# A graph-network kernel's first block held in program order, with fixed steps for projecting, rooting and turning each group of rows

## The chip, the core and the metric

The kernel runs on one core of one Trainium2 chip. The metric is the device time of one execution in microseconds (us), as a median of several. Inside the core five engines work side by side, each through its own queue: TensorE (PE) multiplies matrices, VectorE (DVE) and ScalarE (ACT) work on elements, GpSimd (POOL) does next to nothing here, and SyncE (SP) issues the transfers between main memory and the core's own memory. Results of TensorE land in PSUM[...] from where DVE or ACT take them.

## What is computed

Four layers of graph attention over 3327 nodes with 256 features and one adjacency matrix; each layer is added to its input and normalised. The last layer has three attention stages inside. The change touches only the first layer:

```python
def _L0_gnn_ref(features, adj, Wq, Wk):
    Qn = _cos_normalize(features @ Wq.T)     # rows of 128, divided by their length
    Kn = _cos_normalize(features @ Wk.T)
    raw_att = Kn @ Qn.T
    att = jnp.where(adj > 0, raw_att, NEG) * TEMP
    att = jax.nn.softmax(att, axis=1)
    prop_fea = att @ features
    adj_mask = (jnp.sum(adj, axis=1) > 0).astype(features.dtype)[:, None]
    prop_fea = adj_mask * prop_fea + (1.0 - adj_mask) * features
    return (1.0 - KEEP_RATIO) * prop_fea + KEEP_RATIO * features
...
x = _layernorm(x + _L0_gnn_ref(x, adj, L0_gnn_Wq, L0_gnn_Wk), axis=-1)
```

## The kernel before

**Tiling.** The nodes are padded to 3328 and cut into 26 tiles of 128 (NT) and 7 blocks of 512 (NB; the last has 256). Six layers in the kernel's count (the last layer's three stages apart) each run over blocks b, and inside a block over tiles j (the loop at L908; one turn of it is called a step). Step j of a block multiplies the weights e of tile j (128 rows by the block's 512 columns) with the values V of tile j, in eight matmuls that add up over j in four PSUM tiles `po` (L946). A softmax's denominator comes from a column of ones in V.

**Weights.** They are made two steps ahead (LA = 2) by `make`. For layer 0, `weights0(b, j)` (L429) does, for even j, `take_adj`, which turns two tiles of the adjacency matrix from int32 into a mask of bytes (L386) and adds them to a running sum (L392, L396), and `load_adj`, which loads the next pair into one of three slots called `stage`. Then one product `ps` (L435), its exp on ACT (`ex`, L444), and on DVE exp times mask (`e`, L424). Rows of 128 of the normalised keys and queries, transposed, lie in `FT[g]`: ps for tile j needs half 0 of group g = j // 4 and half 1 of group b.

**Preparing FT.** `prep0(g)` (L280) is a generator that prepares a group of four tiles, and its `yield`s cut it into parts that the loop places:
- projecting: four products `pqk` on PE (16 matmuls, L305), copied to `qk` by DVE or, for groups 1 and 2, ACT (L315, L317);
- squares and their sums (L296 on DVE, L300 on ACT);
- rooting: the inverse square root of eight sums a row by a guess and three Newton steps, twelve short DVE instructions (L328 and `rsqrt`, L130 to L139, result `rn`);
- scaling: half 0 on ACT (L338), half 1 on DVE (L340);
- turning: eight transposes `pqkT` on PE (L346), half 1 before half 0, each half copied into FT on ACT (L350; for group 0 half 1 on DVE, L348).

During block 0 of layer 0 all of this happens between the steps; later blocks find FT complete. `sum_adj` (L400) closes a block's adjacency sum at step 23.

**Order.** A scheduler decides the order of instructions on each engine. Inside a region opened at L68, the instructions of PE, ACT, DVE and POOL stay in the order in which the program states them; SP isn't in the list:

```python
start = tc.manual_schedule(
    engines={engines.PE, engines.Activation, engines.DVE, engines.Pool}
)
```

The region ends after the fourth step (L954). From there on the scheduler may move instructions, such as masks of later tiles, ahead of others, as far as data and slots allow. PSUM has three banks for everything but `po` (tag `pb`), stage has three slots, `e` five and `ex` three, `xT` two.

The parts of a group are placed by the lines L915 to L944: in the third step of four, group g + 1's x is loaded and the group after it projected and squared; in the first two of the next four steps it is rooted with scaling, and turned. The tile that needs a newly turned group first is made one step later.

Of the kernel before, what the change touches and what calls it, by code (L numbers as in the profile page):

```python
# [8 lines left out]
F32 = mybir.dt.float32  # L9
# [8 lines left out]
P = 128  # L18
D = 256
H = 128  # L20
# [11 lines left out]
def gnn_stack(ctx: ExitStack, tc: tile.TileContext, a: dict, N: int, out: bass.AP):  # L32
# [14 lines left out]
    def bw(b):  # L47
        return min(CH, NP - b * CH)
# [227 lines left out]
    def load_x(g):  # L276
        for t in tiles_of(g):
            nc.sync.dma_start(V[0][t][:, :D], a["x"][t * P : (t + 1) * P, :])

    def prep0(g):  # L280

        wd = bw(g)
        xT = xTs[g]
        ts_ = tiles_of(g)
        ss = cols.tile([P, 2, 4], F32, tag="ss", name="ss")
        if len(ts_) < 4:
            nc.vector.memset(ss, 1.0)
        qks = []

        def squares(k):  # L290
            for i in range(2):
                s = qks[k][:, i * H : (i + 1) * H]
                c = ss[:, i, k : k + 1]
                jk = work.tile([P, H], F32, tag=f"sq{i}", name=f"sq{i}", bufs=1)
                if g < 2 and i == 1:
                    nc.vector.tensor_tensor_reduce(  # L296
                        jk, s, s, 1.0, 0.0, ALU.mult, ALU.add, c
                    )
                else:
                    nc.scalar.activation(jk, s, AF.Square, accum_out=c)  # L300

        for k, t in enumerate(ts_):
            pm = bank("pqk")
            for h in range(2):
                nc.tensor.matmul(  # L305
                    pm[:, : 2 * H],
                    xT[:, h, k * P : (k + 1) * P],
                    w["qk"][:, h, :],
                    start=(h == 0),
                    stop=(h == 1),  # L310
                )
            tag, bufs = ("y", 6) if g % 2 else ("qk", 4)
            qk = work.tile([P, 2 * H], F32, tag=tag, name="qk", bufs=bufs)
            if g in (1, 2):
                nc.scalar.copy(qk, pm[:, : 2 * H])  # L315
            else:
                nc.vector.tensor_copy(qk, pm[:, : 2 * H])  # L317
            qks.append(qk)
            if g == 0:
                squares(k)  # L320
        yield
        if g > 0:
            for k in range(len(ts_)):
                squares(k)
            yield

        sf = ss.rearrange("p i k -> p (i k)")
        nc.vector.tensor_scalar(sf, sf, COS_EPS * COS_EPS, None, ALU.max)  # L328
        rn = cols.tile([P, 8], F32, tag="rn", name="rn")
        rsqrt(rn, sf, 8)  # L330
        if g == 1:
            yield
        for k in range(len(ts_)):
            for i in (1, 0):
                s = qks[k][:, i * H : (i + 1) * H]
                c = rn[:, 4 * i + k : 4 * i + k + 1]
                if i == 0:
                    nc.scalar.mul(s, s, c)  # L338
                else:
                    nc.vector.tensor_scalar(s, s, c, None, ALU.mult)  # L340
        yield
        for i in (1, 0):
            pt = bank("pqkT")
            for k, t in enumerate(ts_):
                s = qks[k][:, i * H : (i + 1) * H]
                nc.tensor.transpose(pt[:, k * P : (k + 1) * P], s, ident)  # L346
            if i == 1 and g == 0:
                nc.vector.tensor_copy(FT[g][:, i, :wd], pt[:, :wd])  # L348
            else:
                nc.scalar.copy(FT[g][:, i, :wd], pt[:, :wd])  # L350


    masks = {}
# [4 lines left out]
    def mask(b, j, n=1):  # L358
        wd = bw(b)
        return masks[b][:, j * wd : (j + n) * wd]  # L360
# [21 lines left out]
    def take_adj(b, j):  # L382

        wd = bw(b)
        st = stages.pop((b, j))[:, : 2 * wd]
        nc.vector.tensor_scalar(mask(b, j, 2), st, 0, None, ALU.is_gt)  # L386
        if j == 0:
            adj_sum[b] = st
        elif j == 2:
            acc = work.tile([P, 2 * CH], I32, tag="acc", name="acc", bufs=1)  # L390
            acc = acc[:, : 2 * wd]
            nc.vector.tensor_tensor(acc, adj_sum[b], st, ALU.add)  # L392
            adj_sum[b] = acc
        else:
            acc = adj_sum[b]
            nc.vector.tensor_tensor(acc, acc, st, ALU.add)  # L396
# [24 lines left out]
    def masked(b, j, t_):  # L421
        wd = bw(b)
        e = work.tile([P, CH], F32, tag="e", name="e", bufs=5)
        nc.vector.scalar_tensor_tensor(  # L424
            e[:, :wd], t_[:, :wd], 0.0, mask(b, j), ALU.add, ALU.mult
        )
        return e

    def weights0(b, j):  # L429
        wd = bw(b)  # L430
        if j % 2 == 0:
            take_adj(b, j)
            load_adj()
        ps = bank("ps")
        nc.tensor.matmul(  # L435
            ps[:, :wd],
            FT[j // 4][:, 0, (j % 4) * P : (j % 4 + 1) * P],
            FT[b][:, 1, :wd],
            start=True,
            stop=True,  # L440
        )
        t_ = work.tile([P, CH], F32, tag="a", name="ex", bufs=3)

        nc.scalar.activation(t_[:, :wd], ps[:, :wd], AF.Exp)  # L444
        return masked(b, j, t_)

    gq = {}

# [445 lines left out]
    load_x(0)  # L894
    load_adj()
    masks[0] = new_mask(0)
    prep = [prep0(0), prep0(1)]
    next(prep[0])
    next(prep[1])
    next(prep[0])  # L900
    next(prep[0], None)
    for s in range(LA):
        make(s)
    prep.pop(0)
    setup = setups()
    pre = iter(())

    for s, (L, b, j) in enumerate(steps):  # L908
        last = L.key == "3c"
        first = L.key == "0" and b == 0  # L910
        if j == 0:
            pos = [
                ps_o.tile([P, D + 1], F32, tag="po", name="po") for _ in tiles_of(b)
            ]
        if first:  # L915

            g, part = (j + 4) // 4, j % 4
            if part == 2 and g + 1 < NB:
                load_x(g + 1)
                if g + 2 < NB:  # L920
                    load_xT(g + 2)
                prep.append(prep0(g + 1))
                next(prep[-1])
                if g > 1:
                    next(prep[-1])
                else:
                    next(prep[0])
                    next(prep.pop(0), None)
            if j == 3:
                next(prep[0])  # L930
            if g < NB and g > 1 and part < 2:
                next(prep[0], None)
                if part == 1:
                    prep.pop(0)
        if j == 0 and first:
            load_x(1)
            load_xT(2)
            make(s + LA)
            next(prep[0])
        elif j == 1 and first:  # L940
            make(s + LA)
            next(prep[0])
        else:
            make(s + LA)  # L944
        for k in range(len(pos)):
            nc.tensor.matmul(  # L946
                pos[k],
                made[0][:, k * P : (k + 1) * P],
                V[L.i % 2][j],
                start=(j == 0),  # L950
                stop=(j == NT - 1),
            )
        made.popleft()
        if s == 3:  # L954
            start.__exit__(None, None, None)
        if L.key == "0" and j == NT - 1 - LA:
            sum_adj(b)
        advance()
        if L.key == "0" and b < NB - 1:
            if j == 8:  # L960
                masks[b + 1] = new_mask(b + 1)
        elif j == 8 and not (last and b == NB - 1):
            nb = (b + 1) % NB
            masks[nb] = fetch_mask(nb)
        if L.key == "0" and b >= 1 and j % 3 == 1:
            next(setup, None)
        nl, nb = (L, b + 1)
        if nb == NB:
            nl, nb = (None if last else layers[L.i + 1]), 0
        begin = 14  # L970
        if j == 20:
            while pending:
                advance()
        if nl is not None and nl.key != "0":
            if j == begin:
                pre = ahead(nl, nb)
            if j >= begin:
                next(pre, None)
        if j == NT - 1:
            if b == 0 and not last:  # L980
                nl = layers[L.i + 1]
                L.sum = Sum()
                if nl.is_gat:
                    if nl.key == "1":
                        while "row_1" not in w:
                            next(setup)
                    nl.gat = Gat(nl.key)
                    L.gat_next = nl.gat
            pending.append(finish(L, b, pos))
            advance()  # L990
# [65 lines left out]
```

## Time and profile before

| | |
|---|---|
| median of 3 runs | 2455.1 us (2454.94 to 2455.62) |
| profiled execution | 2453.89 us, of which its span 2452.1 us |
| PE busy in the first 56 us | 47.14 us, mean granted clock 0.94 |
| PE busy from 56 to 112 us | 56.00 us, clock 1.00 |
| PE busy from 112 to 400 us | 288.00 us |
| DMA share, first 56 us and 56 to 112 us | 0.87 and 0.17 |

The span is the time from the first to the last recorded instruction; the execution's own time includes what lies around it. "Busy" counts the time in which an engine had an instruction in work. Block 0 of layer 0 fills about the first 112 us of the span. A timeline line gives the start, the duration, the engine, the line of the code, the operation, the written and read tiles and their shapes, and in brackets the idle time before it with what ended it. A waits line gives who waited for whom, the total in us, the count and the longest. A windows line gives a stretch, its length, the busy time of PE, weight loads, DVE, ACT and POOL, then the granted clock of PE, the busy share of the DMA engines and GB/s.

### The profile page before, as it was taken

How to read it: one execution, taken by the hardware profiler on the slowest of the kernel's cores; microseconds unless marked ns; L12 is line 12 of the kernel's file. 1: busy time of each engine (PE TensorE's matmuls, PEld its weight loads, DVE VectorE, ACT ScalarE, POOL GpSimd, SP SyncE). 2: the span in 40 equal slices, each digit the busy share in tenths (PEclk: the TensorE clock that was granted, in tenths of full speed). 3: DMA queues.
4: the chain of work that ended last, by engine and by line, in shares of the span. 5: the costliest groups of instructions: out<-in, count | busy, mean ns of one | idle time of the engine just before them, and what ended most of it. 6: DMA issues, size and time to landing. Idle time of an engine off the chain costs nothing.

```text
span 2452.1 us, 28282 instructions
## 1 busy us (share of the span) xinstructions
PE 2424.2 (99%) x10373; PEld 1922.1 (78%) x10373; DVE 1411.7 (58%) x3659; ACT 963.5 (39%) x1638; POOL 5.4 (0%) x65
## 2 busy tenths in 40 slices
PE   8999999999999999999999999999999999999997
PEld 6777777788888866666666688888888888888886
DVE  8567777656666634244244256556656555656655
ACT  4422222254444422222222244454554444544443
POOL 0000000000000000000000000000000000000000
PEclk9999999999999999999999999999999999999999
DMA  8135433321110101011010021010010011021110
GB/s 290 63 127 161 140 120 106 109 78 41 41 50 26 65 5 45 5 50 45 1 46 31 1 78 37 33 56 26 33 65 33 33 34 48 33 86 54 58 43 17
DMA packets 53375, 147.92 MB, mean 60 GB/s; under 512 B 6525, under 2 KB 31348, under 8 KB 48628
## 3 DMA queue, kind: packets, MB, share of 16 engines
q1 hardware_dynamic: 52964, 145.85, 17.8%
q8 instruction: 81, 1.33, 0.2%
q14 instruction: 58, 0.48, 0.1%
q10 hardware_dynamic: 272, 0.26, 0.0%
HBM read 124.72 MB, written 21.36 MB: 60 GB/s over the span
## 4 chain that ended last, share of the span: by engine, by line
PE 96%; DVE 2%; ACT 1%; DMA 1%; issue 0%; DVEq 0%; ACTq 0%
PE po L946 70%; PE ps L497 12%; PE ps L435 6%; PE pproj L732 4%; PE pv L815 1%; PE pgq L456 1%; PE ppT L717 1%; PE pqk L305 1%; ACT re L590 0%; DMA stage<-in_adj_a 0%; DVE acc L396 0%; PE pqkT L346 0%; PE pxT L805 0%; DVE mask L386 0%; DVE e L424 0%; DVE e L598 0%
## 5 line engine op out<-in xcount | busy, mean ns | idle before, releaser
L946 PE MATMUL po<-v,e 128*128 128x257 f32 x8112 | 1848.2, 380 | 3.0 <-DVE e L424 1.8
L946 PEld LDWEIGHTS po<-v,e 128*128 128x128 f32 x8112 | 1528.9, 190 | 354.4 <-issue 129.2
L590 ACT ACTIVATE re<-u,nrh,th 128x512 f32<-128x512 f32 (+1 forms) x728 | 562.2, 781 | 593.3 <-DVE e L598 539.5
L598 DVE SCALAR_TENSOR_TENSOR e<-re,rh,mask 128x512 f32<-128x512 f32 (+1 forms) x728 | 515.7, 711 | 466.7 <-PE po L946 454.1
L424 DVE SCALAR_TENSOR_TENSOR e<-ex,mask 128x512 f32<-128x512 f32 (+1 forms) x364 | 236.1, 649 | 443.5 <-ACT ex L505 332.5
L497 PE MATMUL ps<-gT,ft 128*128 128x512 f32 (+1 forms) x728 | 320.4, 562 | 0.0
L505 ACT ACTIVATE ex<-ps,off 128x512 f32<-128x512 f32 (+1 forms) x182 | 119.4, 657 | 399.9 <-PE ps L497 385.4
L497 PEld LDWEIGHTS ps<-gT,ft 128*128 128x128 f32 x728 | 137.2, 190 | 89.9 <-issue 79.4
L444 ACT ACTIVATE ex<-ps 128x512 f32<-128x512 f32 (+1 forms) x182 | 103.1, 567 | 262.1 <-PE ps L435 238.4
L435 PE MATMUL ps<-ft,ft 128*128 128x512 f32 (+1 forms) x312 | 150.2, 565 | 0.7 <-ACT ft L350 0.7
L396 DVE CUSTOM_DVE_ANT_0 acc<-acc,stage 128x2048 uint16<-128x2048 uint16 (+1 forms) x77 | 87.4, 1134 | 0.1
L732 PE MATMUL pproj<-w_l_w,pT 128*128 128x256 f32 x312 | 81.0, 382 | 1.6 <-DVE pT L721 1.5
L386 DVE TENSOR_SCALAR mask<-stage 128x1024 uint8<-128x1024 int32 (+1 forms) x91 | 58.4, 643 | 19.4 <-DMA stage<-in_adj_a 17.3
L742 ACT ACTIVATE elu_e<-elu_e 128x256 f32<-128x256 f32 x130 | 53.0, 408 | 38.5 <-DVE elu_e L741 38.4
L732 PEld LDWEIGHTS pproj<-w_l_w,pT 128*128 128x128 f32 x312 | 58.2, 190 | 11.9 <-DVE pT L721 4.0
L435 PEld LDWEIGHTS ps<-ft,ft 128*128 128x128 f32 x312 | 57.2, 191 | 10.1 <-ACT ft L350 0.9
L703 ACT ACTIVATE p<-po,ri 128x256 f32<-128x256 f32 x130 | 54.1, 465 | 8.3 <-PE po L946 6.5
L618 DVE TENSOR_TENSOR xsum<-xsum,v 128x256 f32<-128x256 f32 (+1 forms) x130 | 54.3, 418 | 1.6
L741 DVE TENSOR_SCALAR elu_e<-pproj 128x256 f32<-128x256 f32 x104 | 43.8, 421 | 6.8 <-PE pproj L732 5.3
L721 DVE COPY pT<-ppT 128x256 f32<-128x256 f32 x104 | 43.1, 414 | 1.1 <-PE ppT L717 1.1
L639 DVE BATCH_NORM_STATS2 bn<-y 128x6 f32<-128x256 f32 x104 | 42.3, 418 | 1.6
L717 PE MATMUL ppT<-ident,p 128*128 128x128 f32 x208 | 39.8, 273 | 0.6 <-ACT p L703 0.6
(146 smaller groups left out, 906.0 us busy)
## 6 DMA issues: line engine op xcount, KB each, us to landing
mask<-mask_d SPq DMA_DIRECT2D x30, 1664.0 KB
stage<-in_adj_a SPq DMA_DIRECT2D x78, 512.0 KB
mask_d<-mask SPq DMA_DIRECT2D x6, 1664.0 KB
u<-s_d SPq DMA_DIRECT2D x24, 256.0 KB
mask<-mask_d SPq DMA_DIRECT2D x5, 832.0 KB
v<-in_x SPq DMA_DIRECT2D x26, 128.0 KB
stage<-in_adj_z SPq DMA_DIRECT2D x13, 256.0 KB
x_d<-o SPq DMA_DIRECT2D x26, 128.0 KB
```

The lines of the kernel that those rows point to most:

```text
L386: nc.vector.tensor_scalar(mask(b, j, 2), st, 0, None, ALU.is_gt)
L396: nc.vector.tensor_tensor(acc, acc, st, ALU.add)
L424: nc.vector.scalar_tensor_tensor(e[:, :wd], t_[:, :wd], 0.0, mask(b, j), ALU.add, ALU.mult)
L435: nc.tensor.matmul(ps[:, :wd], FT[j // 4][:, 0, (j % 4) * P : (j % 4 + 1) * P], FT[b][:, 1, :wd], start=True, stop=True,)
L444: nc.scalar.activation(t_[:, :wd], ps[:, :wd], AF.Exp)
L497: nc.tensor.matmul(ps[:, :wd], FT[j // 4][:, h, (j % 4) * P : (j % 4 + 1) * P], g[:, h, :wd], start=(h == 0), stop=(h == 1),)
L505: nc.scalar.activation(t_[:, :wd], ps[:, :wd], AF.Exp, bias=off, scale=1.0 / D**0.5)
L590: nc.scalar.activation(t_[:, :wd], self.u[b][:, :wd], AF.Relu, bias=self.nrh[:, j : j + 1], scale=self.th[:, j : j + 1],)
L598: nc.vector.scalar_tensor_tensor(e[:, :wd], t_[:, :wd], self.rh[:, j : j + 1], mask(b, j), ALU.add, ALU.mult,)
L717: nc.tensor.transpose(pt[:, h * P : (h + 1) * P], p4[:, k, h * P : (h + 1) * P], ident)
L732: nc.tensor.matmul(pm[:, :D], pT[:, h, :], w[L.w][:, h, :], start=(h == 0), stop=(h == 1),)
L946: nc.tensor.matmul(pos[k], made[0][:, k * P : (k + 1) * P], V[L.i % 2][j], start=(j == 0), stop=(j == NT - 1),)
```

## The change

The ordered region now lasts to the end of block 0 (step NT - 1). `prep0` has five parts for every group, each ended by a `yield`: projecting (with the squares of groups 0 and, for half 0 on ACT, 1), squares, rooting, scaling, turning. In the loop a group has a fixed place within four steps: projected and squared at the end of a step with j % 4 = 3, rooted and scaled in the next but one step behind the making of a tile's weights, and turned in the step after that, ahead of the making of the first tile that needs it. Groups 1 and 2 have places of their own at the start. Loads of x and xT move to the steps with j % 4 = 0. Adding a pair of adjacency tiles to the running sum moves out of `take_adj`, to behind the weights of the tile (`add_adj`).

```diff
-        def squares(k):
-            for i in range(2):
-                s = qks[k][:, i * H : (i + 1) * H]
-                c = ss[:, i, k : k + 1]
-                jk = work.tile([P, H], F32, tag=f"sq{i}", name=f"sq{i}", bufs=1)
-                if g < 2 and i == 1:
...
+        def square(k, i, vector=False):
+            s = qks[k][:, i * H : (i + 1) * H]
+            c = ss[:, i, k : k + 1]
+            jk = work.tile([P, H], F32, tag=f"sq{i}", name=f"sq{i}", bufs=1)
+            if vector:
...
             qks.append(qk)
             if g == 0:
-                squares(k)
-        yield
-        if g > 0:
-            for k in range(len(ts_)):
-                squares(k)
-            yield
+                square(k, 1, True)
+            if g < 2:
+                square(k, 0)
+        yield
+        for k in range(len(ts_)):
+            if g > 1:
+                square(k, 0)
+            if g > 0:
+                square(k, 1, g == 1)
+        yield
...
         rsqrt(rn, sf, 8)
-        if g == 1:
-            yield
+        yield
...
                 nc.scalar.copy(FT[g][:, i, :wd], pt[:, :wd])
+        yield
...
     def take_adj(b, j):
 
         wd = bw(b)
+        st = stages[b, j][:, : 2 * wd]
+        nc.vector.tensor_scalar(mask(b, j, 2), st, 0, None, ALU.is_gt)
+
+    def add_adj(b, j):
+
+        wd = bw(b)
         st = stages.pop((b, j))[:, : 2 * wd]
-        nc.vector.tensor_scalar(mask(b, j, 2), st, 0, None, ALU.is_gt)
         if j == 0:
             adj_sum[b] = st
...
         nc.scalar.activation(t_[:, :wd], ps[:, :wd], AF.Exp)
-        return masked(b, j, t_)
+        e = masked(b, j, t_)
+        if j % 2 == 0:
+            add_adj(b, j)
+        return e
...
-    prep = [prep0(0), prep0(1)]
+    prep = {g: prep0(g) for g in range(NB)}
     next(prep[0])
     next(prep[1])
-    next(prep[0])
-    next(prep[0], None)
+    for _ in range(4):
+        next(prep[0])
+    next(prep[1])
     for s in range(LA):
         make(s)
-    prep.pop(0)
...
         if first:
 
-            g, part = (j + 4) // 4, j % 4
-            if part == 2 and g + 1 < NB:
+            g, part = (j + LA) // 4, j % 4
+            if part == 0 and g + 1 < NB:
                 load_x(g + 1)
                 if g + 2 < NB:
                     load_xT(g + 2)
-                prep.append(prep0(g + 1))
-                next(prep[-1])
-                if g > 1:
-                    next(prep[-1])
-                else:
-                    next(prep[0])
-                    next(prep.pop(0), None)
+            if j < 2:
+                next(prep[1])
+            if j == 2:
+                next(prep[2])
+            if part == 2 and g < NB:
+                next(prep[g])
+        make(s + LA)
+        if first:
+            g = (j + 3) // 4
             if j == 3:
-                next(prep[0])
-            if g < NB and g > 1 and part < 2:
-                next(prep[0], None)
-                if part == 1:
-                    prep.pop(0)
-        if j == 0 and first:
-            load_x(1)
-            load_xT(2)
-            make(s + LA)
-            next(prep[0])
-        elif j == 1 and first:
-            make(s + LA)
-            next(prep[0])
-        else:
-            make(s + LA)
+                next(prep[2])
+            elif part == 1 and j > 1 and g < NB:
+                next(prep[g])
+                next(prep[g])
         for k in range(len(pos)):
             nc.tensor.matmul(
...
         made.popleft()
-        if s == 3:
+        if first and part == 3 and j > 3 and (g := (j + 5) // 4) < NB:
+            next(prep[g])
+            next(prep[g])
+        if s == NT - 1:
             start.__exit__(None, None, None)
```

More of the change, by code (lines that the diff above doesn't have):

```diff
@@ L288, in prep0 @@
         qks = []
-        def squares(k):
-            for i in range(2):
-                s = qks[k][:, i * H : (i + 1) * H]
-                c = ss[:, i, k : k + 1]
-                jk = work.tile([P, H], F32, tag=f"sq{i}", name=f"sq{i}", bufs=1)
-                if g < 2 and i == 1:
-                    nc.vector.tensor_tensor_reduce(
-                        jk, s, s, 1.0, 0.0, ALU.mult, ALU.add, c
-                    )
-                else:
-                    nc.scalar.activation(jk, s, AF.Square, accum_out=c)
+        def square(k, i, vector=False):
[3 more added lines that the diff above has]
+            if vector:
+                nc.vector.tensor_tensor_reduce(
+                    jk, s, s, 1.0, 0.0, ALU.mult, ALU.add, c
+                )
+            else:
+                nc.scalar.activation(jk, s, AF.Square, accum_out=c)
         for k, t in enumerate(ts_):
@@ L921, in gnn_stack @@
                     load_xT(g + 2)
-                prep.append(prep0(g + 1))
-                next(prep[-1])
-                if g > 1:
-                    next(prep[-1])
-                else:
-                    next(prep[0])
-                    next(prep.pop(0), None)
-            if j == 3:
-                next(prep[0])
-            if g < NB and g > 1 and part < 2:
-                next(prep[0], None)
-                if part == 1:
-                    prep.pop(0)
-        if j == 0 and first:
-            load_x(1)
-            load_xT(2)
-            make(s + LA)
-            next(prep[0])
-        elif j == 1 and first:
-            make(s + LA)
-            next(prep[0])
-        else:
-            make(s + LA)
+            if j < 2:
[7 more added lines that the diff above has]
+            g = (j + 3) // 4
+            if j == 3:
+                next(prep[2])
+            elif part == 1 and j > 1 and g < NB:
+                next(prep[g])
+                next(prep[g])
         for k in range(len(pos)):
```

## The prediction

> **What bounds the kernel now.** First the page's busy table and chain: TensorE is busy for nearly the whole span and carries 96% of the chain, so time changes only where TensorE gets or loses a gap, or runs slowly.
>
> ```profile
> PE 2424.2 (99%) x10373; PEld 1922.1 (78%) x10373; DVE 1411.7 (58%) x3659; ACT 963.5 (39%) x1638; POOL 5.4 (0%) x65
> PE 96%; DVE 2%; ACT 1%; DMA 1%; issue 0%; DVEq 0%; ACTq 0%
> ```
>
> Second, the waits of TensorE alone. One row stands out; its longest instance, 6.2 us, is the turning of a group (L346) waiting for its scaling (L340).
>
> ```profile
> PE pqkT L346 <- DVE qk L340: 6.4, 2, 6.2
> PE ps L435 <- ACT ft L350: 1.4, 2, 0.7
> ```
>
> Third, TensorE's timeline around it: the gap lies in the first block, before group 2 is turned, and the work after it is slow.
>
> ```profile
> 34.43 5.36 PE L946 MATMUL po<-v,e 128*128 128x257 f32 x24
> 46.04 1.94 PE L346 MATMUL pqkT<-ident,qk 128*128 128x128 f32 x8 [6.24 <-DVE qk L340]
> 47.77 1.92 PE L435 MATMUL ps<-ft,ft 128*128 128x512 f32 x2
> 49.48 4.85 PE L305 MATMUL pqk<-w_l_wqk,xT 128*128 128x256 f32 x16
> 54.17 1.88 PE L435 MATMUL ps<-ft,ft 128*128 128x512 f32 x4
> ```
>
> Windows of 1 us give the granted clock there (next to last but two columns): half speed until 52 us.
>
> ```profile
> 49.00:50.00 1.00, 1.00 (x3) 0.43 (x2) 0.95 (x1) 0.27 (x1) 0.00 (x0) 0.50 0.99 279
> 53.00:54.00 1.00, 1.00 (x7) 0.86 (x6) 0.97 (x3) 0.89 (x6) 0.00 (x0) 1.00 0.97 348
> ```
>
> VectorE's timeline gives the cause: group 2's root chain starts at 33.55 and ends at 44.56, because masks and sums of later adjacency tiles, some waiting for their transfer, stand between its short instructions.
>
> ```profile
> 33.55 0.17 DVE L328 TENSOR_SCALAR ss<-ss 128x8 f32<-128x8 f32 x1
> ...
> 41.80 0.69 DVE L386 TENSOR_SCALAR mask<-stage 128x1024 uint8<-128x1024 int32 x1 [0.56 <-DMA stage<-in_adj_a]
> ...
> 44.40 0.16 DVE L139 SCALAR_TENSOR_TENSOR rn<-rs_q,rs_y 128x8 f32<-128x8 f32 x1
> ```
>
> From 54.17 to the block's end near 112 us the chain is gapless TensorE work, the turning of groups 3 to 6 included.
>
> [...] VectorE stood 0.56 us before the mask above although the root chain behind it had its data. So an instruction's place in its queue is what counts here. [...] 0.50 after 6.24 us of idling, 1.00 after the shorter gaps of 0.68 us at 15 and 28 us.
>
> **The pitches I use**, all from the chain and the timelines of before: two score matmuls (ps) 0.86 us, eight po matmuls 1.73, projecting a group 3.45, turning one 0.87. One step is ps + po = 2.59. From ps to its weights:
>
> ```profile
> 76.04 1.02 PE L435 MATMUL ps<-ft,ft 128*128 128x512 f32 x2
> 77.10 0.60 ACT L444 ACTIVATE ex<-ps 128x512 f32<-128x512 f32 x1 [0.22 <-PE ps L435]
> 77.73 0.69 DVE L424 SCALAR_TENSOR_TENSOR e<-ex,mask 128x512 f32<-128x512 f32 x1 [2.78 <-ACT ex L444]
> ```
>
> The chain puts this ps at 76.20, so VectorE can start what follows e 2.14 us after ps starts (77.73 + 0.61 - 76.20). Rooting undisturbed, and scaling to the next ps:
>
> ```profile
> 9.93 0.17 DVE L328 TENSOR_SCALAR ss<-ss 128x8 f32<-128x8 f32 x1 [0.20 <-ACT sq L300]
> ...
> 11.95 0.17 DVE L139 SCALAR_TENSOR_TENSOR rn<-rs_q,rs_y 128x8 f32<-128x8 f32 x1
> ```
> ```profile
> 25.95 1.28 ACT L338 ACTIVATE qk<-qk,rn 128x128 f32<-128x128 f32 x4
> 27.14 1.10 ACT L350 COPY ft<-pqkT 128x512 f32<-128x512 f32 x2
> ```
>
> Rooting takes 2.19 us. Scaling on ScalarE starts 0.03 later; from there to the ps behind the turn was 2.34 (25.95 to 28.29). Together 2.4 from the root's end.
>
> **Change, part 1: masks and sums of later tiles leave the root chain.** With the first block in program order, VectorE takes mask(j) at make(j) and add(j) behind its weights. Before lost, against the pitches: 1.8 at the start (12.38 to 15.03 holds 0.87 of turning), 1.9 at group 1 (25.48 to 28.29 holds 0.87), 9.4 at group 2 (39.63 to 54.17 holds 0.87 + 0.86 + 3.45), and 0.2 in crumbs: 13.3 us. The 9.4 has the idle time and the slow clock in it, and this arrangement goes altogether.
>
> **Part 2: the start.** ScalarE squares each tile of group 1 behind its copy. Three fit in the 0.49 us it idled between copies; the last (activate and accumulator read, 0.43 pitch) stands before group 0's scaling, which ends the start chain: +0.45. VectorE's four squares (0.33 each) and the first mask fall into its 2.09 us wait before the first weights: nothing, and at most +0.5 if that cover shrank. Start loss 1.8 + 0.45 + 0.1.
>
> **Part 3: group 1.** Its root (2.19) now comes before mask(2), its scaling before e(3). Counting on: ps(0) 15.5, e(1) done 18.8, root to 20.9, mask(2), e(2) and the first sum to 23.2, scaling to 24.0, well before projecting of group 2 ends at 26.0. Turning then waits for no scaling, but ps(4) needs FT[1], and ScalarE copies both halves first: last transpose to second copy's end leaves 0.9. So 0.9 where 1.9 was.
>
> **Part 4: groups 2 to 6, the new wait.** In each four steps the order is: step 1 ps(j+2), its exp, its e, then rooting and scaling, then po(j); step 2 turning, then ps of the tile that needs exactly this group. With T the start of ps in step 1: VectorE reaches the root at T + 2.14, ends it at T + 4.33, and the next ps can start at T + 6.73. TensorE has po(j) and the turning to do, until T + 3.46. Loss 3.27 each for groups 2 to 5, 13.1 in all. Group 6 has two tiles: scaling 0.69 instead of 1.28 and copies 0.65 instead of 1.10, so the next ps at T + 5.9, against 3.03: 2.9. Sum 16.0. Behind the waiting transpose stand ps and po[...]. Before hid all this for groups 3 to 6, because it turned one step before the tile that needed it (turn, an older ps, po) and had rooted earlier.
> Bounds: if squares or copies are late too, 0.5 more per group; if ScalarE starts the first half's copy during scaling gaps, 0.6 less. So 13 to 18.5.
>
> **Part 5: the block's end.** sum_adj now stays in place: af follows e(25) by 0.69, so is ready at T + 2.95 against po(23)'s end at T + 2.59: 0.4.
>
> **Part 6: transfers.** SP isn't among the ordered engines. Stage slots come free later: the fourth adjacency load waits for the first sum, now at about 23.2 (before, issued at 20.13). It is wanted by mask(6) at some 32.6; loads took about 4 us from issue to mask when VectorE waited (27.77 to 31.80). Later ones have six steps, over 15 us. x and xT loads need no earlier place than before. Cost nothing; if the slack were gone, a microsecond or two once. Block 1 starts with three fewer masks made ahead (3 x 0.6 us on VectorE, 58% busy): nothing, bounded at -1 to +2 because its order is planned anew.
>
> **Sum.** After: 2.35 + 0.9 + 16.0 + 0.4 = 19.6 lost; before 13.3. +6.3 us. The profiled execution took 2453.89 (span 2452.1), giving 2460.2; it lies 1.2 under the median 2455.1, so the forecast for a median is 2461.4, +0.26%.
>
> **Rivals.**
> *Rooting early (faster).* If VectorE in fact roots before e(j+2), from the fixed order being looser than I read it, the root ends by about po's end and only the copies' 0.9 per group remain: 5 x 0.9 + 2.35 + 0.9 + 0.4 = 8.1 lost, -5.2, 2449.9. For it: a mask stands inside group 1's root at 24.14, so the order has holes. Against: that was work from outside the ordered region; inside it TensorE and ScalarE follow the text to the instruction. It decides once rooting ends before T + 2.6.
> *The clock falls at each wait (slower still).* TensorE idles 2 us, turns sparsely for 1.3, idles 0.7. [...] each group pays again what 46 to 52 us paid: ps 1.71 for 0.86, projecting 4.64 for 3.45, part of the turning, about 2.5. +12.5, 2474. Against: 25.57 to 28.29, turning likewise sparse, kept 1.00.
> *No measurable change.* The waits come out nearer 2.5 each, or block 1's new plan gives some back: 13.3 against about 15, 2457.
>
> **How the numbers follow.** Forecast 0.66, clock 0.13, no change 0.09, rooting early 0.12. A measurement tells 0.2%, 4.9 us, from nothing; about a fifth of the forecast's own spread (2457 to 2465) lies within that. Slower 0.66, same 0.22, faster 0.12. Range 2450 to 2472: from the faster rival's figure to short of the full clock penalty, leaving out about half of each.
>
> **What would show it.** Right: the 6.2 us row gone; TensorE waiting about 2 us before L346 five times and about 0.7 before L435 six times; rn ending about 1.7 us after po in those steps; PEclk 1.00 through the block; block 0 ending some 6 us later. Wrong: L346 starting right behind po, rn before e in the queue, mask waiting on stage for microseconds, or a half clock after each turn.

## The result, and the profile after

| | before | after |
|---|---|---|
| median, 6 runs each | 2454.68 us (2454.05 to 2455.62) | 2470.09 us (2467.10 to 2473.09) |
| ratio to before | 1 | 1.0063, 95% interval 1.0050 to 1.0076 |
| profiled execution | 2453.89 us | 2468.12 us |
| PE clock, 0 to 56 and 56 to 112 us | 0.94 and 1.00 | 0.97 and 0.94 |

The change makes the kernel slower by 0.63%, 15.4 us. The forecast was 2461.4 us: the right side and within its range, but only two fifths of the size. On the changed kernel's profile page the busy and chain lines look like those of before; TensorE is still the bound.

```profile
PE 2430.3 (99%) x10373; PEld 1924.6 (78%) x10373; DVE 1414.1 (57%) x3659; ACT 964.5 (39%) x1638; POOL 5.4 (0%) x65
PE 96%; ACT 2%; DVE 1%; DMA 0%; issue 0%; DVEq 0%; ACTq 0%
```

The waits of TensorE (who waited for whom, total us, times, longest us) show what was exchanged: the single wait of 6.2 us is gone, and short ones have come instead, two in each of groups 2 to 6.

```profile
PE pqkT L348 <- DVE qk L342: 8.6, 5, 2.1
PE ps L443 <- ACT ft L352: 4.8, 7, 0.7
PE pqkT L348 <- ACT qk L340: 2.4, 2, 2.2
...
PE pasum L419 <- DVE af L413: 0.4, 1, 0.4
```

Group 5 may stand for groups 2 to 6. First VectorE's timeline (start us, us, engine, line, operation, tiles): the weights e, then at once the root chain, then the scaling.

```profile
96.00 0.69 DVE L432 SCALAR_TENSOR_TENSOR e<-ex,mask 128x512 f32<-128x512 f32 x1 [0.53 <-ACT ex L452]
96.61 0.16 DVE L331 TENSOR_SCALAR ss<-ss 128x8 f32<-128x8 f32 x1
...
98.62 0.17 DVE L139 SCALAR_TENSOR_TENSOR rn<-rs_q,rs_y 128x8 f32<-128x8 f32 x1
98.82 0.87 DVE L342 TENSOR_SCALAR qk<-qk,rn 128x128 f32<-128x128 f32 x4
```

And TensorE's over the same stretch:

```profile
94.32 1.02 PE L443 MATMUL ps<-ft,ft 128*128 128x512 f32 x2
95.17 1.90 PE L948 MATMUL po<-v,e 128*128 128x257 f32 x8
99.17 1.35 PE L348 MATMUL pqkT<-ident,qk 128*128 128x128 f32 x8 [2.10 <-DVE qk L342]
101.25 2.08 PE L443 MATMUL ps<-ft,ft 128*128 128x512 f32 x2 [0.73 <-ACT ft L352]
103.11 2.59 PE L948 MATMUL po<-v,e 128*128 128x257 f32 x8
105.54 1.02 PE L443 MATMUL ps<-ft,ft 128*128 128x512 f32 x2
```

po is done some 2 us before the first scaled tile is there; then the transposes go at the pace of the scaling, and ps waits for both copies. What stands behind is slow as well: ps takes 1.86 us to the next start and po 2.43, where behind the same wait of group 4, shown last, they take 0.97 and 1.73. Windows of 1 us (the granted clock is the last number but two) say why:

```profile
102.00:103.00 1.00, 1.00 (x2) 0.34 (x1) 0.00 (x0) 0.00 (x0) 0.00 (x0) 0.50 0.00 0
105.00:106.00 1.00, 1.00 (x6) 0.68 (x5) 0.81 (x1) 0.00 (x0) 0.00 (x0) 1.00 0.00 0
```

The clock fell to a half behind the waits of groups 2, 3, 5 and 6, and not behind group 4's, which has the same waits:

```profile
80.90 1.35 PE L348 MATMUL pqkT<-ident,qk 128*128 128x128 f32 x8 [2.09 <-DVE qk L342]
82.98 1.12 PE L443 MATMUL ps<-ft,ft 128*128 128x512 f32 x2 [0.73 <-ACT ft L352]
83.95 1.90 PE L948 MATMUL po<-v,e 128*128 128x257 f32 x8
```

### The profile page after: what moved, and what is told of

Read it like the earlier page. It is cut to its first block, busy times and chain, and to the rows that moved or that the text cites. A ratio compares the mean times of both kernels' runs of the same rounds, so it can differ in the third digit from the quotient of the medians.

```text
span 2466.0 us, 28299 instructions
## 1 busy us (share of the span) xinstructions
PE 2430.3 (99%) x10373; PEld 1924.6 (78%) x10373; DVE 1414.1 (57%) x3659; ACT 964.5 (39%) x1638; POOL 5.4 (0%) x65
## 4 chain that ended last, share of the span: by engine, by line
PE 96%; ACT 2%; DVE 1%; DMA 0%; issue 0%; DVEq 0%; ACTq 0%
PE po L948 70%; PE ps L508 12%; PE ps L443 6%; PE pproj L743 4%; PE ppT L728 1%; PE pv L826 1%; PE pqk L304 1%; PE pgq L467 1%; ACT re L601 1%; DMA u<-s_d 0%; ACT ft L352 0%; DVE e L432 0%; PE pxT L816 0%; ACT qk L340 0%; ACT ex L452 0%
## 5 line engine op out<-in xcount | busy, mean ns | idle before, releaser
L389 DVE TENSOR_SCALAR mask<-stage 128x1024 uint8<-128x1024 int32 (+1 forms) x91 | 58.4, 643 | 15.4 <-DMA stage<-in_adj_a 13.8
```

## The experiments

Theory: the program order is a gain, and the fixed places are the loss, by two waits a group and by the slow clock that these bring on. Rivals: the program order itself costs, since every mask and sum now comes just in time; or the clock falls for another reason. All ran beside the kernel before, with 5 to 15 executions each; every ratio is to the kernel before, with its 95% interval.

**1. The changed kernel again.** No edit.

> The changed kernel once more, beside the kernel before on the same chip. Theory (order): the five waits of about 2.1 us before the turning and seven of 0.7 us before ps come again to within 0.1 us, since they follow from the order alone; the share of the slow clock may differ. 12 to 18 us slower than before. Rival (transfers): waits differ in place and length from the first profile.

2471.98 us, ratio 1.0065 (1.0052 to 1.0077).

```profile
PE pqkT L348 <- DVE qk L342: 8.6, 5, 2.1
PE ps L443 <- ACT ft L352: 4.7, 7, 0.7
```

The waits came again to the tenth: they follow from the order. The clock fell in the same four groups in this execution, in groups 2 and 3 for twice as long (6.8 us), and once more at 16.9 us, in the start, which it hadn't in the first profile. This makes the 4.4 us between the two profiled executions (2472.48 and 2468.12): the first po starts 2.2 us later, and 2.3 are added in groups 2 and 3.

**2. Only the longer ordered region, with the places of before.**

```diff
-        if s == 3:
+        if s == NT - 1:
             start.__exit__(None, None, None)
```

> The kernel before with only the ordered region lengthened to the end of the block. Theory (the places cost, not the program order): group 2's root chain loses its masks, the 6.2 us wait and the slow clock behind it go, turning stands one step before the tile that needs it, so no new wait; 7 to 10 us faster than before, about 2446. Rival (program order itself costs, since VectorE then makes every mask and sum just in time): waits of PE on e or on the scaling in most groups, slower than before by 5 us or more.

2447.22 us, 0.9966 (0.9952 to 0.9979). TensorE's timeline at group 2, where the kernel before stood still for 6.24 us:

```profile
34.92 1.90 PE L946 MATMUL po<-v,e 128*128 128x257 f32 x8
36.66 1.24 PE L346 MATMUL pqkT<-ident,qk 128*128 128x128 f32 x8
38.02 1.12 PE L435 MATMUL ps<-ft,ft 128*128 128x512 f32 x2
38.98 1.90 PE L946 MATMUL po<-v,e 128*128 128x257 f32 x8
```

One line of the change, alone, is worth 7.4 us. The rival that program order costs is out. ps follows the turning here without waiting for it, as it works on a tile of the older group.

**3. Only the places, with the short region.** The opposite of run 2.

```diff
-        if s == NT - 1:
+        if s == 3:
             start.__exit__(None, None, None)
```

> The changed kernel with the ordered region ending after the fourth step, as before, so that the scheduler orders the rest. Theory: most of the five waits go, because the scheduler roots and turns early; masks can stand in a root chain again and bring back one wait of several us; between 5 us faster and 8 slower than before. Rival (the places cost whatever the order): five waits of 2 us and 12 or more slower.

2454.14 us, 0.9995 (0.9987 to 1.0003): not to be told from before. VectorE's timeline in group 2 shows masks between the short instructions of the root chain again, which lasts from 37.18 to 45.62 us instead of 2.2 us:

```profile
37.18 0.17 DVE L331 TENSOR_SCALAR ss<-ss 128x8 f32<-128x8 f32 x1
...
42.97 0.69 DVE L389 TENSOR_SCALAR mask<-stage 128x1024 uint8<-128x1024 int32 x1
43.57 0.16 DVE L136 TENSOR_TENSOR rs_q<-rs_y 128x8 f32<-128x8 f32 x1
43.64 1.22 DVE L404 CUSTOM_DVE_ANT_0 acc<-acc,stage 128x2048 uint16<-128x2048 uint16 x1
...
45.46 0.16 DVE L139 SCALAR_TENSOR_TENSOR rn<-rs_q,rs_y 128x8 f32<-128x8 f32 x1
```

In later groups the scheduler put po between the turning and the ps that needs it, so waits for the scaling are left in groups 2 and 3 alone (2.54 and 0.81 us), and in the start. The clock fell behind group 2's, for 6.8 us. The five waits of the changed kernel need both, the places and the held order.

**4. The wait filled.** Further transposes, whose results are overwritten; nothing else is computed with them.

```diff
             pt = bank("pqkT")
+            if g > 1 and i == 1:
+                for _ in range(18):
+                    nc.tensor.transpose(pt[:, :P], ident, ident)
```

> The changed kernel with 18 further transposes of the identity (about 1.96 us, into the bank that the real transposes then overwrite) ahead of the turning of groups 2 to 6. Theory (the idle wait makes the clock fall): the wait of 2.1 us is filled to about 0.1, the clock stays at 1.00 in the block, and the time is 5 to 10 us below the changed kernel's, about 6 over before. Rival (the clock falls for another reason, or the wait only moves): clock falls as often, and the time is equal to the changed kernel's or up to 10 us over it.

2461.93 us, 1.0033 (1.0022 to 1.0043), an interval apart from that of run 1. TensorE at group 5, and a window over it:

```profile
93.06 2.13 PE L348 MATMUL pqkT<-ident 128*128 128x128 f32 x18
95.33 1.35 PE L351 MATMUL pqkT<-ident,qk 128*128 128x128 f32 x8
97.41 1.12 PE L446 MATMUL ps<-ft,ft 128*128 128x512 f32 x2 [0.73 <-ACT ft L355]
98.37 1.90 PE L951 MATMUL po<-v,e 128*128 128x257 f32 x8
```
```profile
93.00:101.00 8.00, 7.13 (x41) 5.26 (x39) 4.95 (x18) 2.95 (x7) 0.00 (x0) 1.00 0.15 56
```

The order is as late as before, since the filling only takes the place of the wait; but ps and po behind it go at full speed in all five groups. So the fall of the clock comes from the idling: with the wait filled the clock is 1.00 in the windows over all five groups. Its cost is read from the two profiled executions, neither of which has a fall in the start: 7.2 us (2468.12 less 2460.95), of which 0.5 is an earlier start. The medians of runs 1 and 4 lie 10.0 apart, but a difference of medians isn't the five groups' alone: run 4's own executions lie in two places, 2461.0 to 2461.9 and 2465.0 to 2465.4, and falls elsewhere, as in run 1's start, may be what parts them.

**5. Rooting and scaling at the start of the step before**, turning where the change put it.

```diff
+            if part == 0 and 4 <= j and (j + 4) // 4 < NB:
+                next(prep[(j + 4) // 4])
+                next(prep[(j + 4) // 4])
         make(s + LA)
         if first:
-            g = (j + 3) // 4
             if j == 3:
                 next(prep[2])
-            elif part == 1 and j > 1 and g < NB:
-                next(prep[g])
-                next(prep[g])
```

> The changed kernel with groups 2 to 6 rooted and scaled one step earlier, at the start of the step with j % 4 = 0, ahead of the weights made there. Theory: scaling is over before TensorE comes to the turning, so the waits of 2.1 us go and the clock stays at 1.00; the 0.7 us waits of ps on the copies stay, seven of them. Lost 8 us instead of 13.3 before: about 5 us faster than before. Rival (the wait only moves, since e is now late behind rooting): waits of po on e, no faster than before.

2449.87 us, 0.9983 (0.9975 to 0.9990). TensorE at group 3:

```profile
53.98 1.04 PE L348 MATMUL pqkT<-ident,qk 128*128 128x128 f32 x8
55.75 1.12 PE L443 MATMUL ps<-ft,ft 128*128 128x512 f32 x2 [0.73 <-ACT ft L352]
```

The turning finds its tiles scaled; the wait for the copies stays, and the clock stays up. Moving one pair of calls from one step to the one before turns a loss of 15 to 17 us into a gain of 4.8, with no new wait of po.

**6. po ahead of the making of the tile that needs the turned group**, rooting where the change put it.

```diff
-        make(s + LA)
+        late = first and j % 4 == 2 and j > 2
+        if not late:
+            make(s + LA)
...
                 stop=(j == NT - 1),
             )
+        if late:
+            make(s + LA)
```

> The changed kernel with po(j) ahead of the making of tile j + 2 in the steps that turn groups 2 to 6, rooting where the change put it. Theory: the 0.7 us waits of ps on the copies go for these groups, hidden by po; the waits of 2.1 us before the turning stay. 4 us below the changed kernel if the clock falls as often, 10 below if the sparse turning and second wait behind the 2.1 us were needed to make it fall; 5 to 12 us over before. Rival (ps late makes e late): new waits of po on e.

2461.02 us, 1.0027 (1.0016 to 1.0038). Windows over the turning of groups 2 and 3:

```profile
42.00:48.00 6.00, 4.91 (x17) 4.09 (x18) 2.00 (x9) 2.45 (x6) 0.00 (x0) 0.72 0.38 109
60.00:68.00 8.00, 6.06 (x27) 4.56 (x28) 4.25 (x15) 3.55 (x8) 0.00 (x0) 1.00 0.11 46
```

The waits of 2.1 us are all there, those for the copies gone in these groups, and in this execution the clock fell in group 2 alone instead of in four of five (and once in the start). So the 2.1 us and the sparse transposes mostly weren't enough: the second wait behind them belonged to it. The sum's transposes waited 1.3 us here instead of 0.4, because ps(24) now comes later.

**7. Both edits of runs 5 and 6.**

> Both of these edits together. Theory: no wait longer than 0.4 us from group 2 on, clock 1.00; what is left is the start (2.4), group 1 (0.9) and the sum's transposes (0.4), so some 9 us faster than before, 2445 to 2447. Rival: as fast as only one of the two.

2447.22 us, 0.9967 (0.9954 to 0.9979). At group 3 nothing waits:

```profile
53.13 1.04 PE L348 MATMUL pqkT<-ident,qk 128*128 128x128 f32 x8
54.19 1.97 PE L949 MATMUL po<-v,e 128*128 128x257 f32 x8
56.00 1.88 PE L443 MATMUL ps<-ft,ft 128*128 128x512 f32 x4
```

The median is that of run 2: one changed line with the places of before does as well, as far as these executions tell.

**8. The same with group 1 earlier**: rooted and scaled in step 0, turned ahead of the projecting of group 2.

```diff
-            if j < 2:
+            if j == 0:
+                next(prep[1])
                 next(prep[1])
-            if j == 2:
-                next(prep[2])
             if part == 2 and g < NB:
                 next(prep[g])
+            if j == 2:
+                next(prep[2])
```

> The same with group 1 rooted and scaled in step 0 and turned in step 2 ahead of projecting group 2, so that its copies lie under that projecting. Theory: 0.5 to 1 us faster than with both edits. Rival: its scaling is late for the turning or e(2) for po(2), and it is equal or slower by up to 1 us; a difference this small may not be measurable.

2445.74 us, 0.9963 (0.9950 to 0.9977). The wait for group 1's copies is gone, but the median's 1.5 us against run 7 lie within the spread of either (2444.8 to 2448.8 here): not decided. The profiled execution, 2448.81, was the slowest of the five; its clock had fallen in the start, and once more at 478 us, in the last block of the first layer, behind a wait of 1.8 us for e.

**9. Half the filling**: range(9) instead of range(18) in run 4.

> The changed kernel with 9 instead of 18 further transposes of the identity (about 1 us) ahead of the turning of groups 2 to 6. Theory [...]: with 1.1 us of the wait left, the clock falls in 0 to 2 of the 5 groups, and the time is that of the full filling, about 2462, to 4 us over it. Rival (any wait of about a us suffices): it falls in 3 or more, about 2470.

2466.16 us, 1.0044 (1.0031 to 1.0057). In the profile 1.1 us of waiting remain in each group, and ps comes at full speed behind every one:

```profile
97.92 1.35 PE L351 MATMUL pqkT<-ident,qk 128*128 128x128 f32 x8 [1.12 <-DVE qk L342]
100.00 1.12 PE L446 MATMUL ps<-ft,ft 128*128 128x512 f32 x2 [0.73 <-ACT ft L355]
```

No fall in five groups, one in the start and one at 494 us. The median is 4 us over that of the full filling, the end of what was expected. It isn't lost in the groups: in the profiled execution, 2466.16 us and so the median itself, the first po starts 2.60 us later than in run 4's (20.84 against 18.24), and the sum's transposes behind all five groups 2.59 later (121.61 against 119.02). Run 4's profile has neither of the two falls. In this execution half the filling kept the clock up as well as all of it.

**10. Run 8 with the start filled**: one further transpose ahead of each of group 0's half 0, five ahead of the first ps; their results are overwritten.

```diff
+                if g == 0 and i == 0:
+                    nc.tensor.transpose(pt[:, k * P : (k + 1) * P], ident, ident)
...
         ps = bank("ps")
+        if b == 0 and j == 0:
+            for _ in range(5):
+                nc.tensor.transpose(ps[:, :P], ident, ident)
```

> The kernel with both edits and the early group 1, with 9 further transposes of the identity in the waits of the start (one ahead of each transpose of group 0's half 0, five ahead of the first ps). Theory: in some executions the clock falls at about 16 us because of the start's idle stretches; filled, it stays up, and the times lie close together at 2445 or a little over. Rival: the start's clock falls as before, and the times spread over 4 us.

2445.22 us, 0.9959 (0.9945 to 0.9972), with all five runs between 2444.80 and 2445.43. The first six ps matmuls, in run 8's profile and then in this one:

```profile
16.94 4.54 PE L443 MATMUL ps<-ft 128*128 128x512 f32 x6 [0.68 <-ACT ft L352]
```
```profile
16.60 2.84 PE L448 MATMUL ps<-ft 128*128 128x512 f32 x6
```

Nine transposes of about 0.1 us each, in time that was idle anyway, take out the fall in the start, 1.70 us in these lines. With them the spread went from 4 us to 0.6, but not by the start alone: run 8's profiled execution also lost 1.7 us in its fall at 478 us, which run 10's hadn't, and where run 10 changes nothing. That none of five executions shows such a loss may be chance. This is the best kernel of the study.

## Why the prediction came out as it did

*Part 1, masks out of the root chain: right.* The wait of 6.2 us and the slow clock behind it are gone; run 2, which has this part without the new places, gains 7.4 us of the 9.4 that it could; of the rest, its turnings of groups 2 to 5 take 1.14 to 1.36 us to the next ps instead of 0.87 (1.3 in all), and the sum's transposes wait 0.4. Its profile also has a fall of the clock at 476 us (mean clock 0.997, with 1.00 over the first 200 us).

*Part 2, the start: right.* From the first projecting to the first ps it is 10.14 us (5.96 to 16.10) against 9.72 before: +0.42 where 0.45 was forecast. That the first projecting itself began 0.65 us later is not the change's: in other kernels' profiles with the same start it ranged from 5.35 to 6.33.

*Part 3, group 1: right.* 26.55 to 28.32 less 0.87 of turning is 0.9, as forecast.

*Part 4, the new wait: right in place and kind, 0.3 us short in size.* The steps up to the next ps are right: in group 5 the chain puts ps at 94.48, so the root should have ended at 98.81 and the next ps started at 101.21; they did at 98.80 and 101.25. What the sum left out is that a ps behind a wait takes 1.13 us in the chain until po, and not 0.86. In group 4, where the clock stayed up, two steps take 9.62 us (ps at 76.06 to ps at 85.68) for 6.05 of work: 3.57 lost where 3.27 was forecast. Times five this is 1.5 us. For group 6 the text's own figures, scaling shorter by 0.59 and copies by 0.45, give T + 5.7 and not its T + 5.9; measured were 5.94, so this figure came out right by luck.

*Part 5, the sum: right,* 0.4. *Part 6, transfers: right;* up to 125 us no mask waited for a transfer, where before six had.

*What failed is the choice at the clock.* The prediction held that it would stay up, "Against: 25.57 to 28.29, turning likewise sparse, kept 1.00", and gave its fall a chance of 0.13. That stretch was a weak witness: it had paced transposes and one wait of 0.68 us, and no 2 us of standing still ahead of them. In run 4, without the long wait, the clock was 1.00 over all five groups, and in run 6, without the second one, over four of the five: it was mostly the whole stretch of wait, sparse turning and wait with which it fell. The price was mis-sized too: 2.5 us a fall was forecast, and the profile has 1.65, 1.69, 1.59 and 1.48 (ps and po behind the turning, less 0.97 and 1.73 as in group 4), 6.4 in all.

With it block 0 adds up: 6.3 forecast, 1.5 from the longer waits, 6.4 from the clock and 0.65 from the later start make 14.85; the last po of the block starts 14.78 later (129.84 against 115.06). Some 0.9 of this comes back in later layers, so the spans differ by 13.9. In run 4, in which the clock is held, that po is 7.9 late (122.94), and 1.2 come back later: that its profiled execution, 2460.95, lies so near the 2460.2 worked out for a clock that stays up is in part luck.

That the measured median lies inside 2450 to 2472 doesn't speak for the sum behind 2461.4: the range reached so far up only because it took in about half of what the clock rival stood for.

*The rivals.* Rooting early didn't happen by itself, but run 5 put it in by hand: 2449.87, where 2449.9 had been worked out, though its profile has a fall of the clock at 479 us (mean clock 0.997, with 1.00 over the first 200 us) that this figure didn't count. No measurable change was wrong.

## What to carry to other kernels

Holding a stretch in program order is worth having only with places that give each link of a chain its time: add up what stands between two uses of the engine that bounds (here ps, exp, e, root, scale, turn, copy: 6.9 us) against the work that it has in the meantime (3.5 us), and move the early links up until the second is longer. An idle wait on TensorE has to be priced with the clock too: here a wait of 2.1 us cost 3.6 as order, with all that stands behind it, and in four of five groups 1.5 to 1.7 more by the clock. Where a wait can't be removed, cheap matmuls whose result is thrown away can buy the second part back, as run 4's 18 transposes a group did.

## What the runs showed of the hardware

In the changed kernel's profile TensorE's clock went to 0.50 at 43.08, 63.56, 101.10 and 118.17 us, for 3.41 us each time. In groups 2 to 5 TensorE had stood 2.1 to 2.2 us, turned sparsely for 1.3 and stood 0.7; in group 6, with half the turning, these were 2.1, 0.7 and 0.5. The clock fell in four of these five groups, in one of five with 2.1 us of standing and sparse turning alone (run 6), and in none with 1.1 and 0.7 (run 9), 0.7 alone (run 5) or 0.7 with the long wait filled (run 4).

Why equal waits had unequal outcomes isn't shown. The stretches of groups 4 and 5 in the changed kernel, from the last po to ps:

```profile
78.81:82.98 4.17, 1.36 (x9) 0.96 (x8) 2.92 (x14) 2.35 (x6) 0.00 (x0) 1.00 0.27 104
97.07:101.25 4.18, 1.36 (x10) 0.96 (x9) 2.92 (x14) 2.36 (x6) 0.00 (x0) 0.98 0.27 102
```

Both hold 1.36 us of work in 4.2 us. In group 5 the clock fell at 101.10, still ahead of ps; behind group 4's it stayed at 1.00. Nor does the fall come at one place: it is 0.05, 0.15 and 0.39 us ahead of ps in groups 2, 5 and 6, and 0.52 us behind the start of ps in group 3. So the waits and the work of a stretch don't settle by themselves whether the clock falls. In run 9, group 5's stretch holds 2.5 us of work in 4.35 (95.65 to 100.00, less 1.12 and 0.73 of waiting), and none of the five such stretches had a fall; how much less would have done was not measured.

The start's waits, 13.0 to 16.1 us in the changed kernel's first profile, had a fall in some executions and not in others: the six ps behind them took 4.51 to 4.54 us in the profiles of runs 1, 3, 6, 8 and 9, and 2.84 in the others. The waits in the last block of the first layer, 1.77 and 0.67 us around 476 us in run 8's profile, are another such stretch. Each fall there cost 1.7 us, and the two together make 3.4 of the 3.6 us between the profiled executions of runs 8 and 10.
